# Correlation blocks of a convolution: gram matmuls in 32-column groups, two blocks per visit, and columns turned on VectorE

## The chip, the core and the metric

The kernel runs on one core of a Trainium2 chip. Time is device microseconds of one launch that processes all eight images: 2574.16 us, the median of three runs (2573.71 to 2581.83). One further execution was taken with the hardware profiler; the lines and times below come from it, in microseconds from its first instruction.

## The reference, cut to what matters

Two layers act on x of shape (8, 768, 32, 32). The first is a group norm, an attention whose scores come from the variances of keys and values, a projection and a residual. The second is a group norm, a convolution of 1x1 over the 768 channels and 28 correlation channels, and a residual. The change lies in the correlation channels:

```python
norm = jnp.sqrt(jnp.sum(feature * feature, axis=1, keepdims=True))
feat_n = feature / jnp.maximum(norm, EPS)
feat_pad = jnp.pad(feat_n, ((0, 0), (0, 0), (PAD, PAD), (PAD, PAD)))
corr = jnp.stack([jnp.sum(feat_pad[:, :, r:h + r, cc:w + cc] * feat_n, axis=1) for r, cc in _offsets()], axis=1)
x = jnp.concatenate([feature, corr], axis=1)
out = jnp.einsum('bchw,oc->bohw', x, conv_w) + conv_b[None, :, None, None]
```

For each pixel and each of 28 offsets (at most three rows and three columns away), corr is the dot product over 768 channels of the pixel's normalised feature with the neighbour's. Opposite offsets give the same products in another place, so 12 offsets and the pixel with itself are enough.

## The kernel before, in words

The program is written out in full when it is built, one instruction stream for each engine. The order is set by a planner: `Clock` keeps a modelled time, `later.after(us, job)` puts a job at a due time, `pass_time` runs what has come due, and every unit of TensorE work is emitted with its cost in microseconds (`KV_US` 1.93, `T_US` 2.58, `GRAM_US` 1.4). The planner only orders instructions; the engines wait for each other by semaphores, and each engine keeps its order. All loads and stores after the first go through SP's queue.

`work_off` mixes three sources: `rest` (units of the key and value projection of one image and the convolution of the image before), the attention steps (16 pairs of matmuls each, 6.9 us), and `beside`, which holds the correlation's gram blocks. A gram block is taken from `beside` by `next_to`, before and after each attention step and at places put into `rest`; `remaining` takes what is left before the last units of a projection. The wide products are made of matmuls with 64 weight columns, two side by side (`halves`, line 350), at seven products for eight.

The correlation of image b (class `Corr`, lines 1125 to 1254) runs in this order:

- `turn(t)`, lines 1128 to 1141: GpSimd copies block t of 128 tokens (four image rows) of f into a tile with the left and the right 16 columns of the image apart. Two operations a block. The pool `turnpool` has one buffer. Image 7 uses ScalarE and another pool.
- `gram(t)`, lines 1143 to 1180: for each of 6 channel chunks and each side, a matmul of 64 tokens (weights) with a window of 7 rows by 19 columns of the image, 133 moving columns; the last block has 4 rows, 76 columns. In float32 each matmul is two records in the trace. Then a copy to `win` by VectorE (ScalarE for image 7) and two DMAs a block into `windowed` in DRAM, whose row pitch makes the diagonals straight.
- `diagonals`, after blocks 3 and 7 (a half, 512 tokens): four DMAs bring the needed diagonals into `dd`.
- `scale`: norms (VectorE and GpSimd), then 20 columns for each of four blocks of 128 tokens, in `dn`.
- `to_dram` (line 1216 on): `dn` is turned by two TensorE products with an identity (`turned`, line 353, tile ct), copied by VectorE to `cr`, and stored to `rows` by four DMAs.
- `gather` (line 1231 on), after the second half: shifted copies of the rows come into `cs` and `v`, VectorE multiplies them, three DMAs copy the result to four groups of partitions, and `("cs", b)` is ready. `Wide.join` (line 1062) then adds the correlation's part to the convolution's products; image 7 has separate products for it (line 1373).

`KeysValues.spread(half)` (from line 704) makes the attention's scales after a half of the projection: small VectorE operations, one reduction over partitions on GpSimd, then rows to DRAM. At the start, `keep_warm` issues matmuls on an identity while the first image loads.

Of the kernel before, what the change touches and what calls it, by code (L numbers as in the profile page):

```python
# [27 lines left out]
RUNS = ((0, 0, 4), (31, -1, 3), (62, -2, 5), (93, -3, 7))  # L28
HW = W // 2
TALL, WIDE = MT // 2 + 3, HW + 3  # L30
AHEAD_OF = [o for first, _, count in RUNS for o in range(first, first + count)][1:]
NA = len(AHEAD_OF)
PAD = 99
# [20 lines left out]
TAIL = 0.0  # L54
EXP, SUM, STEP_US = 1.07, 1.15, 1.73
KV_US, T_US, CORR_US = 1.93, 2.58, 1.2
GRAM_US = 1.4
WARM, BRIDGE = 38, (3, 6)

# [32 lines left out]
class Clock:  # L92


    def __init__(self):
        self.now, self.count, self.jobs = 0.0, 0, []
        self.act, self.rows, self.poll = 0.0, ([], []), lambda: None
        self.dve = 0.0

    def after(self, us, job):  # L100
        self.count += 1
# [71 lines left out]
def two_layers(ctx, tc, x, wkv, wproj, bproj, wconv, wcorr, bconv, out):  # L173
# [14 lines left out]
    bcpool = pool("bcpool", 4)  # L188
    bkpool = pool("bkpool", 2)
    expool = pool("expool", 2 * AHEAD)  # L190
    turnpool = pool("turnpool", 1)
    wk = pool("wk", 3)
    uvpool = pool("uvpool", 1)
    st = pool("st", 1)
    xbank = pool("xbank", 2, space=PSUM)
    ybank = pool("ybank", 2, space=PSUM)
# [16 lines left out]
    def small(name):  # L213
        return other([P, 512], name)
# [238 lines left out]
    wins = [const.tile([P, WIN], F32, name=f"win{i}") for i in range(3)]  # L453
    for win in wins:
        nc.gpsimd.memset(win, 0.0)
    across = const.tile([W, NA], F32, name="across")

    def mask_rows():
        nc.gpsimd.memset(mask, 1.0)
# [135 lines left out]
    class KeysValues:  # L595
# [48 lines left out]
        def unit(self, half, d, n, g, p):  # L644
            b = self.b
            if n == 0:
                self.make_sums(half, (2 * d, 2 * d + 1))
            s = self.sums[g]
            a = {1: self.block(g, 0, 0), 2: self.block(g, 0, 1), 4: self.block(g, 1, 1)}
            a.update({5: s[:, 0], 6: s[:, 1], 7: s[:, 2], 3: s[:, 3]})  # L650
            w = kv_stream.tiles[b, half, d, p]
            pairs = [(a[p][:, k, :], w[:, k, :]) for k in range(JH)]
            taken = lambda ps: self.take(half, g, p, ps)
            if p == 2 and not b + half + d:
                ps = other([P, KW], f"z{g}")
                for k, (lhsT, rhs) in enumerate(pairs):
                    halves(ps, lhsT, rhs, start=k == 0, stop=k == len(pairs) - 1)
                later.after(KV_US + 0.1, lambda: taken(ps))
            else:
                banks.product(g, p, KV_US, KW, pairs, taken)  # L660
            if p not in [q for _, q in (PAIR if b + half + d else OPENING)[n + 1 :]]:
                kv_stream.done((b, half, d, p))
            if d == 1 and n == len(PAIR) - 1:
                self.over = half == 1
                more = 4.0 if half and not b else 0.0
                later.after(KV_US + 0.5 + more, lambda: later.after_dve(0.0, lambda: self.spread(half)))

        def stats(self, kind, half, t, src):
# [455 lines left out]
    class Corr:  # L1124
# [3 lines left out]
        def turn(self, t):  # L1128
# [7 lines left out]
            for side in range(2):  # L1136
                if last:
                    act_copy(0.5, to[:, :, side], rows[:, :, :, side, :])
                else:
                    half = rows[:, :, :, side, :]  # L1140
                    nc.gpsimd.tensor_tensor(to[:, :, side], half, windows(ones, ones.ap[0], (0, J), (HW, 4), (1, HW)), ALU.mult)  # L1141

        def gram(self, t):

            b = self.b
            tall = min(TALL, H - 4 * t)
            n = tall * WIDE
            if t not in self.turned:
                self.turn(t)
            block = self.turned[t]  # L1150
            ps = other([P, SPAN], f"gr{b}_{t}")
            for j in range(J):
                image = self.f[:, j, :].rearrange("p (y x) -> p y x", x=W)
                for side in range(2):
                    left = side * (HW - 3)
                    nc.tensor.matmul(  # L1156
                        ps[side * HD : (side + 1) * HD, :n].rearrange("p (y x) -> p y x", x=WIDE),
                        lhsT=block[:, j, side, :],
                        rhs=image[:, 4 * t : 4 * t + tall, left : left + WIDE],
                        start=j == 0, stop=j == J - 1,  # L1160
                    )
            for ahead in range(t + 1, min(t + (3 if b == NB - 1 else 2), MT)):
                if ahead not in self.turned:
                    self.turn(ahead)

            def out():
                win = wins[t % 2 if t < MT - 1 else 2]
                if b < NB - 1:
                    vector.tensor_copy(win[:, :n], ps[:, :n])
                else:  # L1170
                    act_copy(0.3, win[:, :n], ps[:, :n])
                for side in range(2):
                    to = windowed[b % 2][t : t + 1, side * (HD * PITCH + HD - 3) :]
                    nc.sync.dma_start(
                        out=windows(to, (HW * PITCH - 3, 4), (PITCH, HW), (1, WIN)), in_=win[side * HD : (side + 1) * HD, :]
                    )
                if t % 4 == 3:
                    later.after(4.0, lambda: self.diagonals(t // 4))

            later.after(GRAM_US + 0.25, out)  # L1180

        def diagonals(self, hf):

# [3 lines left out]
            for down, (_, right, count) in enumerate(RUNS):  # L1187
# [5 lines left out]
                    ),  # L1193
                )
                at += count
            later.after(6.0, lambda: self.scale(hf, dd))

        def scale(self, hf, dd):

# [4 lines left out]
            nc.gpsimd.tensor_tensor(rn, m, neghalf, ALU.pow)  # L1204

            def columns():
                dn = st.tile([P, 4, NROW], F32, tag="dn", name=f"dn{b}_{hf}")
                vector.tensor_copy(dn[:, :, 0], rn)
                for q in range(4):
                    vector.scalar_tensor_tensor(dn[:, q, 1:NROW], dd[:, q, :], rn[:, q : q + 1], mask, ALU.mult, ALU.mult)  # L1210
                later.after_dve(0.7 if b else 5.0 if hf else 7.5, lambda: to_dram(dn))

            def to_dram(dn):
                pt = small(f"ct{b}_{hf}")
                columns, over = dn.rearrange("p q r -> p (q r)"), 4 * NROW - HD
                turned(pt[0:HD, 0:P], columns[:, 0:HD])
                turned(pt[HD:P, 0:P], columns[:, over:])
                cr = work([P, P], f"cr{b}_{hf}")
                vector.tensor_copy(
                    cr.rearrange("k (y s x) -> k y s x", y=4, s=2),  # L1220
                    pt[:, 0:P].rearrange("k (s y x) -> k y s x", s=2, y=4),
                )
                for q in range(4):
                    at, row = PAD + hf * HF + q * P, q * NROW + (HD - over) * (q == 3)
                    nc.sync.dma_start(out=rows[b % 2][:, at : at + P], in_=cr[row : row + NROW, :])
                if hf == 1:
                    later.after(3.0, self.gather)

# [2 lines left out]
        def gather(self):  # L1231

            b, r = self.b, rows[self.b % 2]
            u = cs.rearrange("p a n -> p (a n)")[0:NCH, 0:N]
            v = uvpool.tile([NCH, N], F32, tag="uv", name=f"v{b}")
            nc.sync.dma_start(out=v[NS:NCH, :], in_=windows(r[0:1, PAD:], (0, NS + 4), (1, N)))
            nc.sync.dma_start(out=u[2 * NS : NCH, :], in_=windows(r[1:2, PAD:], (0, 4), (1, N)))
            for n, (first, apart) in enumerate(PICKED):
                k, row = 3 * n, 2 + AHEAD_OF.index(first)
                nc.sync.dma_start(out=u[k : k + 3, :], in_=windows(r[row : row + 1, PAD:], (apart * ROW, 3), (1, N)))  # L1240
                nc.sync.dma_start(out=v[k : k + 3, :], in_=windows(r[0:1, PAD + first :], (apart, 3), (1, N)))
                nc.sync.dma_start(
                    out=u[NS + k : NS + k + 3, :],
                    in_=windows(r[row : row + 1, PAD - first :], (apart * (ROW - 1), 3), (1, N)),
                )

            def product():
                vector.tensor_tensor(u, u, v, ALU.mult)
                vector.tensor_tensor(cs[0:NCH, 2, :], cs[0:NCH, 0, :], cs[0:NCH, 1, :], ALU.subtract)
                for n in range(1, 4):  # L1250
                    nc.sync.dma_start(out=cs[n * FOUR : n * FOUR + NCH, :, :], in_=cs[0:NCH, :, :])
                later.after_dve(6.0, lambda: ready.add(("cs", b)))

            later.after(18.0 if b < NB - 1 else 12.0, product)

    class Conv:

# [133 lines left out]

    def remaining(beside):
        while beside:
            next_to(beside)

    def next_to(beside):

        if beside and ready.issuperset(beside[0][1]):
            us, _, unit = beside.pop(0)
            unit()  # L1400
            clock.pass_time(us)
# [146 lines left out]
    for b in range(NB + 1):  # L1548
# [8 lines left out]
        if b:  # L1557
# [8 lines left out]
            if b < NB:  # L1566
# [6 lines left out]
            grams = [(GRAM_US if t < MT - 1 else 0.9, has_f if b > 1 else has_f + ("turned",), lambda t=t: (corr or corrs[0]).gram(t)) for t in range(MT)]  # L1573
# [71 lines left out]
```

## Time and profile before

| | us |
|---|---|
| median of three runs | 2574.16 |
| profiled execution | 2576.79 |
| its span, first to last instruction | 2575.1 |
| gram records (tile gr), 1536: TensorE busy | 103.49 |
| column turns (tile ct), 64: TensorE busy | 8.72 |
| denominators (tile den), 200: TensorE busy | 26.64 |
| GpSimd's turns, 112 of 384 elements | 110.7 |
| SP, windowed stores, 128: median of one issue | 0.52 |

The granted TensorE clock is full throughout. A row's busy time is the union of its records, and TensorE's records overlap: a matmul's record lasts from its start to a modelled end, while the next one starts long before that. What work takes away from TensorE's stream is therefore read from the starts in the timeline, not from busy times or means.

### The profile page before, as it was taken

The page shows a single profiled execution, that of the slowest core. Times are in us where ns is not written, and L with a number is a line of the kernel's source. Part 1 is how long each engine was busy: PE and PEld are TensorE (multiplying, and loading weights), DVE is VectorE, ACT ScalarE, POOL GpSimd, SP SyncE. Part 2 cuts the span into 40 slices and gives each one's busy share as a digit, 9 for nine tenths or more (in the row PEclk, how much of TensorE's full clock was granted, in tenths as well). Part 3 has the DMA queues.
Part 4 walks back from the last instruction along what each step waited for, and adds up shares of the span by engine and source line. Part 5 has one row for each costly group of instructions (what it writes and reads, how often), then busy time and mean ns, then how long its engine had stood idle before and what let it go on. Part 6 is the DMA issues. An engine that isn't in the chain of part 4 may idle for free.

```text
span 2575.1 us, 40595 instructions
## 1 busy us (share of the span) xinstructions
PE 2566.3 (100%) x14694; PEld 1246.2 (48%) x14694; DVE 1582.3 (61%) x4125; ACT 1417.5 (55%) x1972; POOL 422.4 (16%) x449
## 2 busy tenths in 40 slices
PE   9999999999999999999999999999999999999999
PEld 6545356334554347633476434664344333475333
DVE  6868735775447853478534785358853587535764
ACT  1497279811697217971179711897118971199610
POOL 4320130004300043000430003300133001331000
PEclk9999999999999999999999999999999999999999
DMA  8766366355563655636556365563655636445333
GB/s 293 293 220 229 102 212 186 120 198 170 185 190 116 198 168 178 205 98 206 169 176 202 97 212 169 168 204 100 218 166 174 207 107 218 151 158 167 119 109 109
DMA packets 331818, 448.56 MB, mean 174 GB/s; under 512 B 68431, under 2 KB 252623, under 8 KB 331619
## 3 DMA queue, kind: packets, MB, share of 16 engines
q1 hardware_dynamic: 329554, 442.62, 53.8%
q10 hardware_dynamic: 2064, 3.34, 0.4%
q8 instruction: 117, 1.92, 0.3%
q14 instruction: 83, 0.67, 0.1%
HBM read 376.70 MB, written 64.78 MB: 171 GB/s over the span
## 4 chain that ended last, share of the span: by engine, by line
PE 96%; DMA 2%; ACT 1%; DVE 1%; SPq 0%; issue 0%; POOL 0%; ACTq 0%; POOLq 0%; DVEq 0%
PE x L350 34%; PE av L801 25%; PE y L350 17%; PE z L350 10%; PE own L350 5%; PE gr L1156 3%; PE den L832 1%; ACT ex L775 1%; ACT junk L785 0%; DMA bk<-kdr 0%; DMA kv<-in_wkv_dram 0%; PE z L1062 0%; PE cc L1275 0%; PE y L1062 0%; DVE acc L167 0%
## 5 line engine op out<-in xcount | busy, mean ns | idle before, releaser
L775 ACT ACTIVATE ex<-bc,nk 128x1024 f32<-128x1024 f32 x768 | 826.9, 1139 | 382.4 <-DMA bc<-vdr 256.7
L801 PE MATMUL av<-ex,v 128*64 128x512 f32 x3072 | 699.8, 593 | 0.3 <-ACT ex L775 0.2
L801 PEld LDWEIGHTS av<-ex,v 128*64 128x64 f32 x3072 | 303.8, 137 | 355.3 <-issue 262.0
L785 ACT ACTIVATE junk<-bk,vm 128x1024 bf16<-128x1024 f32 x368 | 421.4, 1145 | 41.5 <-issue 17.8
L167 DVE TENSOR_TENSOR acc<-acc,ex 128x1024 f32<-128x1024 f32 x300 | 344.7, 1216 | 0.0
L350 PE MATMUL y<-kv,s 128*64 128x384 f32 x1488 | 265.6, 487 | 0.9 <-POOL s L636 0.9
L350 PE MATMUL x<-kv,xn 128*64 128x384 f32 x1512 | 261.4, 486 | 0.3 <-DMA kv<-in_wkv_dram 0.3
L350 PE MATMUL x<-kv,s 128*64 128x384 f32 x1488 | 256.2, 486 | 0.0
L229 ACT COPY kp<-x 128x384 f32<-128x384 f32 x28 | 13.4, 479 | 404.8 <-PE x L350 396.0
L350 PEld LDWEIGHTS x<-kv,xn 128*64 128x64 f32 x1512 | 134.2, 137 | 109.9 <-issue 83.9
L350 PEld LDWEIGHTS x<-kv,s 128*64 128x64 f32 x1488 | 131.6, 137 | 108.0 <-issue 87.1
L350 PEld LDWEIGHTS y<-kv,s 128*64 128x64 f32 x1488 | 130.1, 137 | 99.6 <-issue 75.3
L530 POOL TENSOR_TENSOR rstda<-vea,neghalf 128x1 f32<-128x1 f32 x8 | 4.8, 596 | 949.1 <-DVE vea L167 949.1
L1141 POOL TENSOR_TENSOR turn<-f,ones 128x384 f32<-128x384 f32 x112 | 110.7, 1010 | 242.1 <-PE gr L1156 182.2
L350 PE MATMUL z<-kv,xn 128*64 128x384 f32 x768 | 135.4, 486 | 0.0
L350 PE MATMUL x<-f,wt 128*64 128x512 f32 x504 | 120.0, 593 | 0.0
L167 DVE TENSOR_TENSOR v<-y,v 128x128 f32<-128x128 f32 x180 | 41.0, 283 | 124.1 <-PE y L350 124.1
L636 POOL TENSOR_TENSOR s<-xn 128x384 f32<-128x384 f32 x64 | 65.6, 1035 | 294.8 <-PE x L350 183.0
L167 DVE BATCH_NORM_STATS2 vbn<-v 128x6 f32<-128x64 f32 x720 | 101.7, 211 | 0.0
L167 DVE SCALAR_TENSOR_TENSOR xn<-x,bconv_sb,xn 128x512 f32<-128x512 f32 x63 | 46.5, 747 | 89.1 <-PE x L350 86.1
L229 ACT COPY acc<-li 32x256 f32<-32x256 f32 x128 | 51.6, 403 | 82.9 <-DVE li L167 81.5
L350 PEld LDWEIGHTS z<-kv,xn 128*64 128x64 f32 x768 | 72.6, 137 | 49.9 <-issue 36.0
(199 smaller groups left out, 3126.2 us busy)
## 6 DMA issues: line engine op xcount, KB each, us to landing
kv<-kvs SPq DMA_DIRECT2D x124, 576.0 KB
kv<-in_wkv_dram SPq DMA_DIRECT2D x95, 576.0 KB
bc<-vdr SPq DMA_DIRECT2D x96, 512.0 KB
f<-in_x_dram SPq DMA_DIRECT2D x48, 512.0 KB
bk<-kdr SPq DMA_DIRECT2D x46, 512.0 KB
x1d<-f SPq DMA_DIRECT2D x42, 512.0 KB
xn<-x1d SPq DMA_DIRECT2D x42, 512.0 KB
out_dram<-xn SPq DMA_DIRECT2D x82, 256.0 KB
```

Source lines behind the costliest of these rows:

```text
L167: return getattr(self.engine, name)(*args, **kw)
L229: nc.scalar.copy(to, at)
L350: nc.tensor.matmul(out[at], lhsT=lhsT[:, at], rhs=rhs, start=start, stop=stop, **kw)
L530: nc.gpsimd.tensor_tensor(self.rstd, ve, neghalf[:, 0:1], ALU.pow)
L636: nc.gpsimd.tensor_tensor(self.sums[g][:, 0], a[g][2], a[g][3], ALU.add)
L775: nc.scalar.activation(ex, self.bc[e], AF.Exp, scale=self.kv.nk[self.half][:, h, t : t + 1])
L785: nc.scalar.activation(junk, self.bk[e], AF.Exp, scale=self.kv.m2[self.half][:, h, t : t + 1], accum_out=self.sums[:, e, t : t + 1],)
L801: nc.tensor.matmul(self.av[hf][e * HD : (e + 1) * HD, :], lhsT=self.vt[:, t, e, :], rhs=exs[e][:, hf * HF : (hf + 1) * HF], start=t == 0, ...
L832: nc.tensor.matmul(den[at * 32 : (at + 1) * 32, :], lhsT=ones[:, 0:32], rhs=self.acc[e][:, hf * HF : (hf + 1) * HF], start=True, stop=True,)
L1141: nc.gpsimd.tensor_tensor(to[:, :, side], half, windows(ones, ones.ap[0], (0, J), (HW, 4), (1, HW)), ALU.mult)
L1156: nc.tensor.matmul(ps[side * HD : (side + 1) * HD, :n].rearrange("p (y x) -> p y x", x=WIDE), lhsT=block[:, j, side, :], rhs=image[:, 4 * ...
```

## The change

The gram of images 0 to 6 goes from two groups of 64 tokens to four of 32 tokens (two image rows by 16 columns), each with its own window of 5 rows by 19 columns (95 columns); in the last block all four take the same 4 rows. Image 7 keeps two groups. Blocks go two in a row (`grams`), with a gate in the planner (`clock.turned`) that holds the next pair until 5.8 us after the start of the last. Four DMAs store a block's windows where two did (two still in the last block). `turnpool` has two buffers, and both first blocks are turned when the correlation starts.

`dn` becomes a constant tile of 128 columns, four groups of 32; VectorE's 32 by 32 block transpose makes `cr` from it, so TensorE's two products and the copy out of PSUM go. Eight DMAs store a half's rows where four did. `v` is in two tiles, taken from `turnpool`, and loaded with twice the DMAs. The delays of `scale`, `to_dram` and the product are set anew, so is the place of image 0's second `spread` (8 us later), and there are five more warm matmuls at the start.

```diff
-GRAM_US = 1.4
-WARM, BRIDGE = 38, (3, 6)
+GRAM_US, TURN_US = (1.3, 2.4), 3.4
+WARM, BRIDGE = 42, (3, 7)
...
-                more = 4.0 if half and not b else 0.0
+                more = 12.0 if half and not b else 0.0
...
+        def grams(self, t):
+
+            clock.turned = clock.now + GRAM_US[1] + TURN_US
+            for n in range(2):
+                self.gram(t + n)
+
         def gram(self, t):
 
             b = self.b
-            tall = min(TALL, H - 4 * t)
+            last = t == MT - 1
+            groups = 2 if b == NB - 1 else 4
+            tall = min(SHORT if groups == 4 else TALL, H - 4 * t)
...
-                for side in range(2):
-                    left = side * (HW - 3)
+                each = P // groups
+                for at in range(groups):
+                    side, low = divmod(at, groups // 2)
+                    left, first = side * (HW - 3), 4 * t + (0 if last else 2 * low)
                     nc.tensor.matmul(
-                        ps[side * HD : (side + 1) * HD, :n].rearrange("p (y x) -> p y x", x=WIDE),
-                        lhsT=block[:, j, side, :],
-                        rhs=image[:, 4 * t : 4 * t + tall, left : left + WIDE],
+                        ps[at * each : (at + 1) * each, :n].rearrange("p (y x) -> p y x", x=WIDE),
+                        lhsT=block[:, j, side, low * each : (low + 1) * each],
+                        rhs=image[:, first : first + tall, left : left + WIDE],
                         start=j == 0, stop=j == J - 1,
                     )
-            for ahead in range(t + 1, min(t + (3 if b == NB - 1 else 2), MT)):
+            for ahead in range(t + 1, min(t + 3, MT)):
...
-                win = wins[t % 2 if t < MT - 1 else 2]
+                win = wins[t % 3 if t < MT - 1 else 3]
...
-                for side in range(2):
-                    to = windowed[b % 2][t : t + 1, side * (HD * PITCH + HD - 3) :]
+                whole = last or groups == 2
+                size, count, down = (WIN, 4, 0) if whole else (SHORT * WIDE + 3, 2, 2 * (HW * PITCH - 3 + WIDE))
+                for first in range(0, P, count * HW):
+                    side, low = divmod(first, HD)
+                    to = windowed[b % 2][t : t + 1, side * (HD * PITCH + HD - 3) + (down if low else 0) :]
                     nc.sync.dma_start(
...
-            later.after(GRAM_US + 0.25, out)
+            later.after(1.65 if b == NB - 1 else GRAM_US[t % 2] + 0.25, out)
...
-            later.after(6.0, lambda: self.scale(hf, dd))
+            later.after(13.0 if b < NB - 1 else 6.0, lambda: self.scale(hf, dd))
...
-                later.after_dve(0.7 if b else 5.0 if hf else 7.5, lambda: to_dram(dn))
+                later.after_dve(0.7 if b == NB - 1 else (5.0 if hf else 7.0) if b else 3.0 if hf else 6.0, lambda: to_dram(dn))
 
             def to_dram(dn):
-                pt = small(f"ct{b}_{hf}")
-                columns, over = dn.rearrange("p q r -> p (q r)"), 4 * NROW - HD
-                turned(pt[0:HD, 0:P], columns[:, 0:HD])
-                turned(pt[HD:P, 0:P], columns[:, over:])
                 cr = work([P, P], f"cr{b}_{hf}")
-                vector.tensor_copy(
...
+                vector.transpose(cr, dn.rearrange("p q r -> p (q r)"))
+                turned = cr.rearrange("p (q y x) -> p q y x", q=4, y=2)
+                for part in range(4):
+                    s, low = divmod(part, 2)
+                    for y in range(2):
+                        at = PAD + hf * HF + (2 * low + y) * W + s * HW
+                        nc.sync.dma_start(
+                            out=windows(rows[b % 2][0:1, at:], (ROW, NROW), (P, 4), (1, HW)),
+                            in_=turned[32 * part : 32 * part + NROW, :, y, :],
+                        )
...
-            v = uvpool.tile([NCH, N], F32, tag="uv", name=f"v{b}")
-            nc.sync.dma_start(out=v[NS:NCH, :], in_=windows(r[0:1, PAD:], (0, NS + 4), (1, N)))
+            vs = [turnpool.tile([P, J * P], F32, tag="turn", name=f"v{b}_{hf}") for hf in range(2)]
+            for hf, v in enumerate(vs):
+                nc.sync.dma_start(out=v[NS:NCH, :HF], in_=windows(r[0:1, PAD + hf * HF :], (0, NS + 4), (1, HF)))
...
-            later.after(18.0 if b < NB - 1 else 12.0, product)
+            later.after(20.0 if b < NB - 1 else 14.0, product)
...
     def remaining(beside):
         while beside:
+            clock.turned = 0.0
             next_to(beside)
...
-        if beside and ready.issuperset(beside[0][1]):
+        if beside and ready.issuperset(beside[0][1]) and clock.now >= clock.turned:
...
-        later.after(6.0, lambda: ready.add("turned"))
+        later.after(8.0, lambda: ready.add("turned"))
...
         corrs[-1].turn(0)
+        corrs[-1].turn(1)
...
-                for n in (3, 7) if b > 1 else (7, 11, 15):
+                for n in (3, 7) if b > 1 else (7,) + tuple(range(12, 30, 2)):
```

More of the change, by code (lines that the diff above doesn't have):

```diff
@@ L30 @@
 TALL, WIDE = MT // 2 + 3, HW + 3
+SHORT = 2 + 3
 AHEAD_OF = [o for first, _, count in RUNS for o in range(first, first + count)][1:]
@@ L97, in __init__ @@
         self.act, self.rows, self.poll = 0.0, ([], []), lambda: None
-        self.dve = 0.0
+        self.dve = self.turned = 0.0
     def after(self, us, job):
@@ L190, in two_layers @@
     expool = pool("expool", 2 * AHEAD)
-    turnpool = pool("turnpool", 1)
+    turnpool = pool("turnpool", 2)
     wk = pool("wk", 3)
-    uvpool = pool("uvpool", 1)
     st = pool("st", 1)
@@ L452, in two_layers @@
     windowed = [dconst.tile([MT, P * (PITCH + 2)], F32, name=f"windowed{i}") for i in range(2)]
-    wins = [const.tile([P, WIN], F32, name=f"win{i}") for i in range(3)]
+    wins = [const.tile([P, WIN], F32, name=f"win{i}") for i in range(4)]
     for win in wins:
@@ L456, in two_layers @@
     across = const.tile([W, NA], F32, name="across")
+    dns = [const.tile([P, 4, 32], F32, name=f"dn{n}") for n in range(2)]
+    for dn in dns:
+        nc.gpsimd.memset(dn, 0.0)
     def mask_rows():
@@ L1171, in out @@
                     act_copy(0.3, win[:, :n], ps[:, :n])
-                for side in range(2):
-                    to = windowed[b % 2][t : t + 1, side * (HD * PITCH + HD - 3) :]
+                whole = last or groups == 2
[3 more added lines that the diff above has]
+                    to = windowed[b % 2][t : t + 1, side * (HD * PITCH + HD - 3) + (down if low else 0) :]
                     nc.sync.dma_start(
-                        out=windows(to, (HW * PITCH - 3, 4), (PITCH, HW), (1, WIN)), in_=win[side * HD : (side + 1) * HD, :]
+                        out=windows(to, (HW * PITCH - 3, count), (PITCH, HW), (1, size)),
+                        in_=win[first : first + count * HW, :size],
                     )
@@ L1206, in columns @@
             def columns():
-                dn = st.tile([P, 4, NROW], F32, tag="dn", name=f"dn{b}_{hf}")
+                dn = dns[hf]
                 vector.tensor_copy(dn[:, :, 0], rn)
@@ L1210, in columns @@
                     vector.scalar_tensor_tensor(dn[:, q, 1:NROW], dd[:, q, :], rn[:, q : q + 1], mask, ALU.mult, ALU.mult)
-                later.after_dve(0.7 if b else 5.0 if hf else 7.5, lambda: to_dram(dn))
+                later.after_dve(0.7 if b == NB - 1 else (5.0 if hf else 7.0) if b else 3.0 if hf else 6.0, lambda: to_dram(dn))
             def to_dram(dn):
-                pt = small(f"ct{b}_{hf}")
-                columns, over = dn.rearrange("p q r -> p (q r)"), 4 * NROW - HD
-                turned(pt[0:HD, 0:P], columns[:, 0:HD])
-                turned(pt[HD:P, 0:P], columns[:, over:])
                 cr = work([P, P], f"cr{b}_{hf}")
-                vector.tensor_copy(
[L1220 to L1225, printed above, removed]
+                vector.transpose(cr, dn.rearrange("p q r -> p (q r)"))
[8 more added lines that the diff above has]
+                        )
                 if hf == 1:
@@ L1240, in gather @@
                 nc.sync.dma_start(out=u[k : k + 3, :], in_=windows(r[row : row + 1, PAD:], (apart * ROW, 3), (1, N)))
-                nc.sync.dma_start(out=v[k : k + 3, :], in_=windows(r[0:1, PAD + first :], (apart, 3), (1, N)))
+                for hf, v in enumerate(vs):
+                    nc.sync.dma_start(out=v[k : k + 3, :HF], in_=windows(r[0:1, PAD + first + hf * HF :], (apart, 3), (1, HF)))
                 nc.sync.dma_start(
@@ L1247, in product @@
             def product():
-                vector.tensor_tensor(u, u, v, ALU.mult)
+                for hf, v in enumerate(vs):
+                    vector.tensor_tensor(cs[0:NCH, hf, :], cs[0:NCH, hf, :], v[0:NCH, :HF], ALU.mult)
                 vector.tensor_tensor(cs[0:NCH, 2, :], cs[0:NCH, 0, :], cs[0:NCH, 1, :], ALU.subtract)
@@ L1572, in two_layers @@
                 conv.then = low_residual
-            grams = [(GRAM_US if t < MT - 1 else 0.9, has_f if b > 1 else has_f + ("turned",), lambda t=t: (corr or corrs[0]).gram(t)) for t in range(MT)]
+            if b < NB:
+                keys = has_f if b > 1 else has_f + ("turned",)
+                grams = [(GRAM_US[1], keys, lambda t=t: (corr or corrs[0]).grams(t)) for t in range(0, MT, 2)]
+            else:
+                grams = [(1.4 if t < MT - 1 else 0.9, has_f, lambda t=t: corr.gram(t)) for t in range(MT)]
             first, start = (0.0, has_f, conv.sums.first), (0.0, (), conv.start)
```

## The prediction

> **What bounds the kernel.** First the page's busy shares, then its chain of waits: is one engine the bound, and with what? (Engine, busy us, share of the span, instructions; then the chain's shares by engine and by line.)
>
> ```profile
> PE 2566.3 (100%) x14694; PEld 1246.2 (48%) x14694; DVE 1582.3 (61%) x4125; ACT 1417.5 (55%) x1972; POOL 422.4 (16%) x449
> ...
> PE 96%; DMA 2%; ACT 1%; DVE 1%; SPq 0%; issue 0%; POOL 0%; ACTq 0%; POOLq 0%; DVEq 0%
> ```
>
> TensorE holds the whole chain, so every microsecond of matmul stream taken out of it counts and work on other engines counts only where TensorE comes to wait. What a matmul occupies is not its row's mean (278 ns for a gram matmul), since matmuls overlap, but the distance between starts. That is read from the timeline of image 1's correlation (start, duration, engine, line, operation, count):
>
> ```profile
> 655.96 4.04 PE L350 MATMUL x<-kv,s 128*64 128x384 f32 x24
> 659.83 1.59 PE L1156 MATMUL gr<-f,turn 128*64 128x133 f32 x24
> 661.19 2.16 PE L350 MATMUL y<-kv,s 128*64 128x384 f32 x12
> ...
> 692.55 1.59 PE L1156 MATMUL gr<-f,turn 128*64 128x133 f32 x24
> 693.91 0.45 PE L353 MATMUL ct<-ident,dn 128*64 128x128 f32 x4
> 694.12 2.16 PE L350 MATMUL z<-kv,xn 128*64 128x384 f32 x12
> ...
> 712.03 1.02 PE L1156 MATMUL gr<-f,turn 128*64 128x76 f32 x24
> 712.82 3.45 PE L350 MATMUL x<-kv,s 128*64 128x384 f32 x20
> ```
>
> A gram block costs 661.19 - 659.83 = 1.36 us, the last of an image 0.79, a column turn (ct) 0.21. Each block is 24 matmul records, two column groups side by side: 12 rounds of 0.113 us at 133 columns, 0.066 at 76. The 384-column unit gives 3.87 / 12 = 0.3225 a round. Over the three widths that is 0.00083 us a column and next to nothing fixed: the stream is bound by columns alone, and two groups run at the price of one.
>
> **Gram in four groups (images 0 to 6).** Removed: 7 images x (7 x 1.36 + 0.79) = 72.2 us. Put in: each block is still 12 rounds, now of four groups with 5 rows x 19 = 95 columns: 0.066 + 19 x 0.00083 = 0.082 us a round, 0.98 a block. The last block keeps 76 columns and 0.79. Sum: 7 x (7 x 0.98 + 0.79) = 53.6, **18.6 us less**. This needs four 32-column groups to stream at once. The denominators' matmuls are the row for that, the only 128x32 form before:
>
> ```profile
> 248.45 4.05 PE L350 MATMUL z<-kv,xn 128*64 128x384 f32 x24
> 252.43 1.07 PE L832 MATMUL den<-acc,ones 128*32 128x512 f32 x8
> 253.43 16.28 PE L801 MATMUL av<-ex,v 128*64 128x512 f32 x63
> ```
>
> Eight of them, two rounds, take 253.43 - 252.43 = 1.00 us; two rounds of 512 columns by the law above are 2 x 0.4294 = 0.86. So four groups do run side by side, and 0.14 is lost on the way back to 64-column groups. On the way in, 12 rounds of 384 from 248.45 end at 252.32, and den starts at 252.43: 0.11 more. The first 512-column unit after another den (276.21 to 278.84) takes 2.63 instead of 6 x 0.4294 = 2.58: 0.05. That is 0.30 a visit, more where the two 64-column streams run out of step and one has to wait for the other; I take 0.33, with 0.2 and 0.45 as ends. The change makes the visits in pairs of blocks: 7 x 4 = 28 visits, **9.2 us given back** (5.6 to 12.6).
>
> **A rule that speaks against it.** The row first: den's eight records span 1.07 us, each 0.605 long by its group, second round 0.43 later, so four starts fall within some 0.03 us, below 10 ns each. The new gram needs a start every 0.082 / 4 = 0.0204 us, 96 times in a pair. The Trainium skill (TensorE: Matmul & The Clock Gate, section "Wait — 56ns, not 53.3ns?") says that starts never come closer than about 25 ns however small the matmul; its Part 3 gives about 4 ns between groups packed in one array. The trace bears out the second for four in a burst, and nothing shorter than 33 ns for a sustained run (0.79 / 24). By the first rule a block is 48 x 0.025 = 1.20 us and the gram becomes 7 x 8 x 1.20 + 9.2 = 76.4, **4.2 more** than before; by the row it is 53.6 + 9.2 = 62.8, **9.4 less**. I take the row, because it is the same form of matmul, and keep the rule as a rival.
>
> **Column turns on VectorE.** Sixteen ct of 0.21 us leave TensorE: **3.4 us**. VectorE's 128x128 copy out of PSUM (4.67 us for 16) becomes one 128x128 transpose in SBUF; the nearest row, the 128x32 transpose, takes 0.17 to 0.21 us, and VectorE at 61% has room for anything up to a microsecond. Costed at nothing. One PSUM bank fewer is asked for.
>
> **Transfers.** All on SP. Per image 0 to 6: 7 blocks x 2 more windowed issues at 0.52 us, 8 more rows at 0.32, 5 more v at 0.27, 11 us in 318 us; SP's own instructions fill 856 of 2575 us. What queues behind them are weight loads held five and seven blocks ahead. Hidden; uncovered, it would be a kv load late by a burst (8 windowed issues, 4 us) against five blocks that last two units, 3.9 us, each. The rows' pieces shrink from 512 to 64 bytes, a form the trace lacks; nobody waits for it but the correlation.
>
> **The correlation's due time.** Delays grow by 7.0 before scale, 4.3 before the turn (images 1 to 6, second half) and 2.0 before the product: 13.3 us. In image 1, cs was copied at 756.8 to 759.4 and first read at 778.9, about 19 us of cover. And the pairs come sooner: places that took one block now take two, so at 652.7, about 661, 671 and 680 by the units between them, instead of ending at 712. Nothing is late.
>
> **Turns on GpSimd.** Four operations of 1.01 us now stand together after each pair. The first two can start when the first block ends (1.1 us after the pair's start), so all end at about 5.3; the new gate holds the next pair to 5.8. No wait is added. In image 0 blocks came 3.8 us apart and waited, 0.24 and 0.23 us; the gate ends these: **0.5 less**.
>
> **Image 0's later spread.** It moves eight VectorE operations and a reduction out of the way of the last pieces of image 1's normalisation, which GpSimd's sums and then TensorE stand for. The only wait it can free is
>
> ```profile
> 159.15 2.16 PE L350 MATMUL y<-kv,s 128*64 128x384 f32 x12 [0.89 <-POOL s L636]
> ```
>
> **0.9 less** (0 to 0.9). Its own result is due when pair 3's exponentials begin, about 190; it was at hand near 165, and 8 us later still is.
>
> **Warm-up and tail.** Five more warm matmuls: the first group ended at 12.83 with 13.62 next, and four more end at 13.7; the bridge ends before the weights land at 16.86. **+0.2** (0 to 0.3). Image 7 keeps two groups. Its chain to the last correlation gets 2.0 us longer: copies issued at 2550.1 to 2552.7 come to about 2555, with some 2 to landing, and the first reader stood at 2557.17. **+0.5** (0 to 1.5).
>
> **Sum.** -18.6 + 9.2 - 3.4 - 0.5 - 0.9 + 0.2 + 0.5 = -13.5. The profiled execution took 2576.8 (span 2575.1 and 1.7 around it), giving 2563.3; it lies 2.6 above the median of 2574.2, and the change starts from that median: **2561**. With all ends one way: 2556 to 2566.
>
> **Rivals.** *Issue floor:* 25 ns a start, as above: +4.2 - 3.4 - 1.4 + 0.7 = +0.1, **2574**. For it: no sustained run below 33 ns is seen. Against: den's burst, and matmuls queued behind long ones beforehand. *Turns behind sums (slower):* in image 1 GpSimd spends 696.2 to 703.9 on the four sums of a projection and turns nothing. A turn that queues behind them ends at 1.1 + 7.7 + 4.0 = 12.9 us after its pair, the next pair may come at 8.2, so TensorE waits about 5. Once an image that is 35 us: 2561 + 35 = **2596**; from 3 us an image the change is no faster. Against: by the places above the pairs are done before the sums begin; only image 0 (sums at 375.7) comes within a few microseconds. *The groups do not run side by side* but two at a time: 7 x (7 x 1.96 + 1.58) = 107 + 9 - 72 = +44, **2618**; den's row speaks against it.
>
> **Chances.** A measurement of this kernel tells 0.3% (7.7 us) from no change. Forecast 0.74, issue floor 0.14, turns behind sums 0.09, no packing 0.03. The forecast's own range lies wholly on the faster side, the floor in the middle, the others slower. Range 2556 to 2574: the forecast's own and the floor's.
>
> **What would show it.** Right: gram blocks near 1.0 us from start to start within a pair, about 0.3 lost around each pair, no ct on TensorE, TensorE still without waits. The floor shows as starts 25 ns apart and pairs of 2.7 us; the sums as waits of gram for turn; a late cs as waits of the joined matmuls (L1062 before) for cs.

## The result, and the profile after

The changed kernel takes 2595.77 us in the median of six runs (2592.85 to 2602.11), the kernel before beside it 2576.94 (six runs, 2573.71 to 2581.83). The ratio is 1.0076, with an interval of 1.0066 to 1.0086: slower by 0.8%, where 0.5% faster was forecast. The profiled execution took 2593.92, its span is 2592.2.

First the page: engines with busy us, share and instructions; then the chain of waits by engine and by line.

```profile
PE 2572.7 (99%) x15984; PEld 1080.0 (42%) x15984; DVE 1595.7 (62%) x4133; ACT 1415.5 (55%) x1972; POOL 423.1 (16%) x452
...
PE 90%; ACT 5%; DVE 2%; issue 2%; DMA 1%; SPq 0%; POOL 0%; ACTq 0%; DVEq 0%; POOLq 0%
PE x L350 33%; PE av L804 22%; PE y L350 16%; PE z L350 10%; PE own L350 5%; ACT ex L778 3%; PE gr L1169 2%; ACT junk L788 2%; PE den L835 1%; PE warm L419 1%; DMA bk<-kdr 1%; DVE acc L168 0%; DVE v L168 0%; DVE xn L168 0%; PE z L1065 0%
```

TensorE had 96% of the chain and has 90%; ScalarE went from 1% to 5%. Three names in the last line tell the story before any detail: ex (the attention's exponentials), junk (ScalarE's passes for the denominators, named for their unused output) and the DMA bk<-kdr that feeds them. Then TensorE's waits (for whom, us in all, times, longest):

```profile
PE av L804 <- ACT ex L778: 11.5, 14, 2.3
PE warm L419 <- POOL ident masks.py:199: 1.6, 1, 1.6
PE gr L1169 <- issue: 1.5, 1, 1.5
PE x L350 <- DVE t2o L168: 0.6, 1, 0.6
```

Before, attention (av) waited 0.2 us for the exponentials in the whole span; now it waits 11.5. The line of before:

```profile
PE av L801 <- ACT ex L775: 0.2, 1, 0.2
```

The place is the timeline of image 1, here from its second pair of gram blocks on (start, duration, engine, line, operation, count, wait):

```profile
656.55 4.04 PE L350 MATMUL x<-kv,s 128*64 128x384 f32 x24
660.52 2.17 PE L1169 MATMUL gr<-f,turn 128*32 128x95 f32 x96
662.62 2.16 PE L350 MATMUL y<-kv,s 128*64 128x384 f32 x12
664.61 4.04 PE L350 MATMUL x<-kv,s 128*64 128x384 f32 x24
668.58 2.17 PE L1169 MATMUL gr<-f,turn 128*32 128x95 f32 x96
670.67 5.37 PE L804 MATMUL av<-ex,v 128*64 128x512 f32 x24
677.18 2.97 PE L804 MATMUL av<-ex,v 128*64 128x512 f32 x8 [1.14 <-ACT ex L778]
680.08 1.98 PE L1169 MATMUL gr<-f,turn 128*32 128x95 f32 x96
```

The gram did what was forecast: from 660.52 the next unit after a pair starts 2.10 us later, where two separate blocks took 2.72. Then the first attention step has its 32 matmul records from 670.67 to 680.08, 9.41 us; 16 rounds at 0.4294 are 6.87. In the kernel before, the same step ran from 670.29 to 677.15, 6.86:

```profile
670.29 7.09 PE L801 MATMUL av<-ex,v 128*64 128x512 f32 x32
677.15 1.59 PE L1156 MATMUL gr<-f,turn 128*64 128x133 f32 x24
```

So 2.5 us are lost in one step, and the row names only 1.14 of them as a wait. The single records explain the difference. Each tile of exponentials belongs to one of the pair's two heads, and each head is one of the two 64-column streams. At 677.18 and 677.66 only the first head's stream runs, on the seventh tile, which has just been made. The second stream needs the eighth, which ScalarE makes 1.04 us after the seventh; it starts at 678.22, together with the first stream's next matmul, which stands behind it in TensorE's order. The last two records, at 679.13 and 679.55, are the second stream's alone. **The step ends by its last tile, and the list of waits names only the time in which TensorE is wholly idle**, not the wait of one stream while the other runs.

Over the span, TensorE's stream (every matmul's columns at the law's price) fell by 21.0 us, and yet the span grew by 17.1. So it holds 38.1 us more beyond the stream: 28 visits at 0.29 account for 8.1, and 30 are lost time that the forecast did not have. Most of it is in the attention's matmuls: from their starts to the next units' they take 29.2 us more than their columns' price, where it was 4.2 before.

Why are the exponentials late? SP's queue, in the kernel before and then after, at the same place (start, duration, queue, line, transfer, count):

```profile
656.63 1.10 SPq L1174 DMA_DIRECT2D windowed<-win  x2
657.83 5.05 SPq L593 DMA_DIRECT2D kdr<-rsk  x2
662.93 1.01 SPq L306 DMA_DIRECT2D kv<-in_wkv_dram  x2
664.04 1.10 SPq L1174 DMA_DIRECT2D windowed<-win  x2
665.19 1.10 SPq L764 DMA_DIRECT2D bk<-kdr  x2
```

```profile
656.47 2.84 SPq L1190 DMA_DIRECT2D windowed<-win  x4
659.37 3.97 SPq L596 DMA_DIRECT2D kdr<-rsk  x2
663.44 2.51 SPq L1190 DMA_DIRECT2D windowed<-win  x4
666.06 0.92 SPq L306 DMA_DIRECT2D kv<-in_wkv_dram  x2
667.03 2.56 SPq L1190 DMA_DIRECT2D windowed<-win  x4
669.64 1.00 SPq L767 DMA_DIRECT2D bk<-kdr  x2
```

bk is the row of key scales for the first pair of heads; it goes out 4.45 us later, behind twelve windowed stores, 7.91 us in all, instead of four, 2.20 us. (kdr is where the row lies in DRAM; the second of its two transfers waits for the first to land.) ScalarE, before and then after:

```profile
659.78 6.56 ACT L775 ACTIVATE ex<-bc,nk 128x1024 f32<-128x1024 f32 x6 [27.58 <-DMA bc<-vdr]
671.69 1.15 ACT L785 ACTIVATE junk<-bk,vm 128x1024 bf16<-128x1024 f32 x1 [5.35 <-DMA bk<-kdr]
...
672.84 4.25 ACT L775 ACTIVATE ex<-bc,nk 128x1024 f32<-128x1024 f32 x4
```

```profile
660.92 6.56 ACT L778 ACTIVATE ex<-bc,nk 128x1024 f32<-128x1024 f32 x6 [29.02 <-DMA bc<-vdr]
674.84 1.15 ACT L788 ACTIVATE junk<-bk,vm 128x1024 bf16<-128x1024 f32 x1 [7.36 <-issue]
...
675.99 4.25 ACT L778 ACTIVATE ex<-bc,nk 128x1024 f32<-128x1024 f32 x4
```

ScalarE does six exponentials, then has a denominators' pass in its order, which needs bk. (The row of after calls the wait "issue"; in the trace, the semaphore of bk's first load reaches its count at 674.77, and the pass starts at 674.84.) The seventh exponential stands behind that pass: 675.99 instead of 672.84. TensorE's first step uses eight tiles of exponentials and reaches the seventh at about 675.8. So the chain is: stores, bk, junk, ex, av. The kernel before had some 0.5 us to spare on it: its eighth exponential ended at 675.01, and the matmul that reads it started at 675.50.

### The profile page after: what moved, and what is told of

It is laid out like the page before. It is cut to its first block, busy times and chain, and to the rows that moved or that the text cites. A ratio compares the mean times of both kernels' runs of the same rounds, so it can differ in the third digit from the quotient of the medians.

```text
span 2592.2 us, 43459 instructions
## 1 busy us (share of the span) xinstructions
PE 2572.7 (99%) x15984; PEld 1080.0 (42%) x15984; DVE 1595.7 (62%) x4133; ACT 1415.5 (55%) x1972; POOL 423.1 (16%) x452
## 4 chain that ended last, share of the span: by engine, by line
PE 90%; ACT 5%; DVE 2%; issue 2%; DMA 1%; SPq 0%; POOL 0%; ACTq 0%; DVEq 0%; POOLq 0%
PE x L350 33%; PE av L804 22%; PE y L350 16%; PE z L350 10%; PE own L350 5%; ACT ex L778 3%; PE gr L1169 2%; ACT junk L788 2%; PE den L835 1%; PE warm L419 1%; DMA bk<-kdr 1%; DVE acc L168 0%; DVE v L168 0%; DVE xn L168 0%; PE z L1065 0%
## 5 line engine op out<-in xcount | busy, mean ns | idle before, releaser
L804 PE MATMUL av<-ex,v 128*64 128x512 f32 x3072 | 734.5, 594 | 11.8 <-ACT ex L778 11.5
L804 PEld LDWEIGHTS av<-ex,v 128*64 128x64 f32 x3072 | 237.5, 137 | 464.6 <-issue 380.6
L350 PE MATMUL y<-kv,s 128*64 128x384 f32 x1488 | 276.8, 488 | 0.0
L350 PE MATMUL x<-kv,xn 128*64 128x384 f32 x1512 | 273.5, 486 | 0.0
L350 PE MATMUL x<-kv,s 128*64 128x384 f32 x1488 | 264.0, 486 | 0.0
L350 PEld LDWEIGHTS y<-kv,s 128*64 128x64 f32 x1488 | 124.9, 137 | 105.3 <-issue 89.1
L350 PE MATMUL z<-kv,xn 128*64 128x384 f32 x768 | 140.6, 486 | 0.0
L350 PE MATMUL x<-f,wt 128*64 128x512 f32 x504 | 134.7, 592 | 0.0
```

What stands on the lines that cost most here:

```text
L350: nc.tensor.matmul(out[at], lhsT=lhsT[:, at], rhs=rhs, start=start, stop=stop, **kw)
L804: nc.tensor.matmul(self.av[hf][e * HD : (e + 1) * HD, :], lhsT=self.vt[:, t, e, :], rhs=exs[e][:, hf * HF : (hf + 1) * HF], start=t == 0, ...
```

## The experiments

Two theories stood at the start. *Queue:* the added stores delay bk, as above. *Planner:* the planner's new costs (a pair 2.4, turns 3.4) misplace the work around the pairs. Beside every set of runs the kernel before measured 2576.8 to 2577.6.

**1. bk on another queue.** Everything of the change stays; for images 1 to 7 the first pair's bk loads go through ScalarE's queue.

```diff
-            nc.sync.dma_start(out=bc, in_=windows(...))
+            queue = nc.scalar if kind == "k" and self.hp == 0 and self.b else nc.sync
+            queue.dma_start(out=bc, in_=windows(...))
```

> The changed kernel, but the two loads of the denominators' rows (bk) of the first attention pair go out on ScalarE's own queue instead of SP's. Theory Q (SP's queue): these loads stand behind 12 windowed stores where 4 stood before, ScalarE starts the denominators 3 us later, and TensorE waits about 3.4 us for exponentials in the first two attention steps of each of 7 images; with the loads moved, that goes: 2596 - 24 = about 2572, between 2566 and 2580. Theory P (the planner): it counts 2.4 us for a pair of blocks that takes 2.2, so TensorE runs ahead of the plan and finds the exponentials unfinished; the queue is no matter, and the time stays above 2588.

Measured 2570.50 (13 runs, 2569.62 to 2573.60), ratio to before 0.9972 (0.9963 to 0.9980): 25 us faster than the changed kernel. ScalarE's timeline, with its queue in it:

```profile
663.35 0.81 ACTq L768 DMA_DIRECT2D bk<-kdr  x2
664.20 4.27 ACT L779 ACTIVATE ex<-bc,nk 128x1024 f32<-128x1024 f32 x4 [0.21 <-ACT ex L779]
668.65 1.15 ACT L789 ACTIVATE junk<-bk,vm 128x1024 bf16<-128x1024 f32 x1 [0.17 <-DMA bk<-kdr]
...
673.40 4.26 ACT L779 ACTIVATE ex<-bc,nk 128x1024 f32<-128x1024 f32 x4 [3.52 <-PE av L805]
```

The pass starts at 668.65, and the next exponentials wait for TensorE to free their buffers and no longer for bk. TensorE's waits for exponentials fall from 11.5 us to one:

```profile
PE av L805 <- ACT ex L779: 2.0, 1, 2.0
```

**2. The same in the kernel before** (before_bk_queue), to see whether the queue is a gain of its own.

> A control: the kernel before, with the first pair's bk loads on ScalarE's queue. In the kernel before these loads came in time, so theory Q has no wait to remove: 2577 within 4 us. If the move itself were worth the 25 us that it brought after the change, the time would be near 2552.

2574.45 (12 runs), ratio 0.9993 (0.9985 to 1.0002). No gain that can be told. So the 25 us are what the change had cost, and no gain of the other queue.

**3. The planner's costs.**

```diff
-GRAM_US, TURN_US = (1.3, 2.4), 3.4
+GRAM_US, TURN_US = (1.2, 2.1), 3.7
```

> The changed kernel with the planner's costs set to what the trace shows: 1.2 for the first block, 2.1 for the pair, the gate kept at 5.8 us. Theory P: the order comes right, 2572 to 2585. Theory Q: the stores still stand ahead of the loads, so 2591 to 2600.

2597.06, ratio 1.0076 (1.0061 to 1.0091): as the changed kernel. The waits fall otherwise (av waits 19.7 us, in seven places), but the loss stays. The planner theory falls, as far as these costs go.

**4. Three times the stores in the kernel before.** Each windowed store of images 0 to 6 is issued three times, with the same data to the same place.

```diff
-                for side in range(2):
+                for side in (0, 1) * (3 if b < NB - 1 else 1):
```

> The kernel before, with each windowed store of images 0 to 6 issued three times (the same data to the same place), so that 12 stores stand ahead of the first pair's bk loads as in the changed kernel, and nothing else is changed. Theory Q: these loads go out some 4 us later and TensorE waits as it does after the change: slower by 15 to 25 us, 2592 to 2602. Theory P: nothing to do with the queue, 2577 within 4 us.

2713.49, ratio 1.0527 (1.0511 to 1.0543): far past what was expected, and by another mechanism. SP's waits show it:

```profile
SPq L1174 <- DMA windowed<-win: 243.6, 119, 7.5
```

In this program a store to a place that an earlier one writes waits, by a semaphore, for the earlier one's landing, up to 7.5 us. That measures repeated writes, not three issues, so it decides nothing.

**5 and 6. More stores, disjoint.** The kernel before with its two stores a block cut into six, and into eight, each to a place of its own: 12 and 16 of them ahead of bk. The edit for eight (for six the list is ((0, 2), (2, 1), (3, 1))):

```diff
-                    nc.sync.dma_start(out=windows(to, (HW * PITCH - 3, 4), ...), in_=win[side * HD : (side + 1) * HD, :])
+                    for y, count in ((0, 1), (1, 1), (2, 1), (3, 1)) if b < NB - 1 else ((0, 4),):
+                        at = side * (HD * PITCH + HD - 3) + y * (HW * PITCH - 3)
+                        to, p = windowed[b % 2][t : t + 1, at:], side * HD + y * HW
+                        nc.sync.dma_start(out=windows(to, (HW * PITCH - 3, count), ...), in_=win[p : p + count * HW, :])
```

> The kernel before, with the windows of each block of images 0 to 6 in six stores that don't overlap, where two did it (the same data): 12 stores ahead of the first pair's bk loads, as after the change, but with no store waiting for another, as the three-fold stores did. Theory Q: bk goes out some 4 us later, ScalarE starts the denominators 3 us later, TensorE waits in the first attention steps: slower by 12 to 30 us, 2589 to 2607. If the stores were no matter: 2577 within 4 us.

> The kernel before, with the windows of each block of images 0 to 6 in eight stores that don't overlap (one for each image row and side, the same data): 16 stores ahead of the first pair's bk loads. With six stores a block ScalarE began the denominators 1.2 us later and the time grew by 3 us, as good as nothing; after the change it began 3.4 us later and TensorE waited. Theory Q with a threshold (some 2 us of slack in front of the fourth pair of exponentials): now bk goes out 5 to 6 us later than before, ScalarE starts 3 us later, and the time grows by 12 to 30 us, 2589 to 2607. If the queue costs nothing, or grows evenly with the stores: 2577 to 2583.

Six: 2579.82 (20 runs), ratio 1.0012 (1.0005 to 1.0018), a miss. Eight: 2599.67, ratio 1.0090 (1.0073 to 1.0107), as expected. Times in image 1 (us after the first gram) make one line of the four kernels:

| | stores ahead | bk issued | first junk | seventh ex | av waits, all images |
|---|---|---|---|---|---|
| before | 4 | 12.5 | 19.0 | 20.2 | 0.2 |
| six stores | 12 | 15.0 | 19.5 | 20.7 | 1.0 |
| the change | 12 | 17.2 | 22.4 | 23.5 | 11.5 |
| eight stores | 16 | 17.5 | 22.6 | 23.8 | 13.5 |

TensorE's waits in the two, six first:

```profile
PE av L801 <- ACT ex L775: 1.0, 2, 0.6
```

```profile
PE av L801 <- ACT ex L775: 13.5, 8, 3.1
```

The loss follows the pass, not bk's issue. bk 2.5 us later moves the pass by only 0.5, because the pass there starts 4.5 us after that issue instead of 6.5 (why bk lands sooner stays open), and 0.5 us is about what the kernel before could spare; the run is 3 us longer. bk 5 us later moves the pass by 3.6, and the run is 22 us longer. For bk's issue, what counts is SP's time ahead of it, not the number of stores: the change's twelve take 2.84 + 2.51 + 2.56 = 7.91 us, the twelve of the six-store kernel only 3.14 + 3.12 = 6.26, since most of them are of one image row (median of an issue 0.42 against 0.57), and the two kdr transfers between them, which took 5.05 us before, shrink to 3.97 and 3.27. Stores and kdr together are 7.25 before, 9.53 with six, 11.88 in the change and 12.20 with eight (9.69 and 2.51): 2.3, 4.6 and 5.0 more, which is bk's delay in the table within 0.2. With eight stores and nothing else of the change, the kernel before becomes as slow as the changed one: such a delay of the queue is enough to make the loss.

**7. The turn alone.** The kernel before with VectorE's turn, the constant tile and eight row stores; gram, stores and delays as before.

```diff
-                turned(pt[0:HD, 0:P], columns[:, 0:HD])
-                turned(pt[HD:P, 0:P], columns[:, over:])
...
+                vector.transpose(cr, dn.rearrange("p q r -> p (q r)"))
...
+                        nc.sync.dma_start(out=windows(rows[b % 2][0:1, at:], ...), in_=turned[32 * part : 32 * part + NROW, :, y, :])
```

> The kernel before with one part of the change alone: columns turned by VectorE's block transpose into one constant tile, eight row stores a half, the delays as before. Both theories: TensorE loses 16 times 0.21 us, 3.4 us faster, 2573 to 2574; if the stores of 64-byte pieces were to come late to the gather, the wait would stand at the joined matmuls and the time above 2580.

2584.16 (nine runs), ratio 1.0030 (1.0019 to 1.0042): a miss. SP's queue in image 2's attention, before and then with the turn:

```profile
1069.44 6.70 SPq L593 DMA_DIRECT2D vdr<-rsv  x2
...
1079.48 1.08 SPq L764 DMA_DIRECT2D bc<-vdr  x2
```

```profile
1071.15 9.47 SPq L596 DMA_DIRECT2D vdr<-rsv  x2
...
1083.96 1.08 SPq L767 DMA_DIRECT2D bc<-vdr  x2
```

bc, the row of value scales, goes out 4.5 us later. TensorE itself is 1.7 us behind by then, and vdr's first transfer goes out just as much later; the other 2.77 are vdr's 9.47 us instead of 6.70. Its second transfer waits for the first to land, and that comes 2.3 us after the last landing of the gather's copies in both kernels (1075.54 after 1073.26, and 1080.01 after 1077.77). The gather stands behind the eight row stores (3.49 us together, the four took 1.42) and the transfers after them. So ScalarE starts late, and TensorE waits:

```profile
1109.65 3.86 PE L804 MATMUL av<-ex,v 128*64 128x512 f32 x7 [2.77 <-ACT ex L778]
```

It is another row of the attention that comes late by the same queue, here by a landing. In the change, where scale and turn are due later, this wait is not seen: bk_other_queue's trace has a single wait of av, in image 0.

**8. The turn alone, the gather 9 us later.**

```diff
-                    later.after(3.0, self.gather)
+                    later.after(12.0 if b < NB - 1 else 3.0, self.gather)
```

> The turn alone, as before, but the gather is begun 9 us later (image 7's as before), so that the attention's value rows (vdr) of the second half go out ahead of it on SP's queue and not behind it. If turn_alone lost its 3.4 us and 7 more to that order, the waits of 2.8 to 3.3 us for exponentials go, and the time is 2573 to 2576. If the 64-byte stores themselves are the cost, it stays at 2580 to 2590.

2580.33 (20 runs), ratio 1.0010 (1.0004 to 1.0017). Half right: from image 1's first gram to image 6's it takes 1584.6 us against 1589.6 before, with no wait for exponentials there. But image 0 now loses some 9.6 us, with such waits of 6.3 us in all, the longest 4.1.

**9. The grams alone.** bk_other_queue with its columns turned by TensorE as before (ct, four row stores).

> The changed kernel with bk on ScalarE's queue (2570.5), and the columns turned by TensorE as before, with four row stores a half: what VectorE's turn is worth where nothing is late. By the sum of the prediction 16 times 0.21 us: 3.4 us slower, 2574. If TensorE's time there is covered by waits for ScalarE, within 1.5 us of 2570.5.

2574.87 (12 runs), ratio 0.9991 (0.9982 to 0.9999). Against 2570.50, the turn on VectorE is worth 4.4 us by the medians. The two traces don't show where: the profiled executions took 2572.75 and 2573.60, and from image 1's first gram to image 6's bk_other_queue is only 0.7 us the shorter.

**10. One block a visit.** bk_other_queue with each block as a visit of its own, eight an image, at 1.25 in the planner.

```diff
-                grams = [(GRAM_US[1], keys, lambda t=t: (corr or corrs[0]).grams(t)) for t in range(0, MT, 2)]
+                grams = [(1.25, keys, lambda t=t: (corr or corrs[0]).gram(t)) for t in range(MT)]
```

> The changed kernel with bk on ScalarE's queue (2570.5), and the blocks taken one at a time as before, not in pairs: 28 more visits to the 32-column form. At 0.29 us a visit, as the trace of the changed kernel has it, 8.1 us slower: 2578 to 2579. If going in and out of the form cost nothing, within 2 us of 2570.5.

2661.25, ratio 1.0331 (1.0314 to 1.0349), a miss by 80 us. A single visit costs what was expected (1.12 us from its start to the next unit's, 0.10 ahead of it and 0.05 in the unit after: 0.29 over 0.98), but image 1's last gram comes at 717, where pairs had it at 680. The reading that fits is that with the longer delays the correlation is late, and the convolution's units that stand behind it are missing between the attention steps. TensorE waits for ScalarE:

```profile
PE av L805 <- ACT ex L779: 45.1, 17, 4.1
PE av L805 <- ACT v L229: 8.5, 6, 2.3
```

The halved clock (last section) adds to it; in this trace it lasts 41 us in all. So the pairs matter for when the correlation comes, more than for the visits that they save.

**11. Image 0's later spread taken back.** In the changed kernel, `more = 4.0` as before.

> The changed kernel with image 0's second spread back at its place (4.0 instead of 12.0). The wait of 0.89 us of TensorE for GpSimd's sums near 159 us comes back: 2596.7; within 3 us of the changed kernel in any case.

2594.88, ratio 1.0074 (1.0059 to 1.0089): no difference to the changed kernel. The wait of y for GpSimd's sums, 0.9, comes back in its trace, and the end does not move with it.

**12. Attention steps up to 1 us later.** bk_other_queue stands above the forecast; is TensorE reaching the steps too soon?

```diff
-            return self.made >= self.done + AHEAD and self.exp_at <= clock.now + 1.0
+            return self.made >= self.done + AHEAD and self.exp_at <= clock.now
```

> The changed kernel with the first pair's bk loads on ScalarE's queue (bk_other_queue, 2570.5) and one constant of the planner different: an attention step may start when the planner's own clock says that its exponentials are there, no longer up to 1.0 us before. bk_other_queue stands some 9 us above the forecast sum. If that rest is TensorE reaching the attention steps just ahead of the exponentials, so that its two column streams fall a round out of step, steps that start up to 1.0 us later with projection rounds put ahead of them give 2563 to 2568, and the waits of av for ex (2.0 us in all) go. If the rest is that the projection rounds run out ahead of the steps, pushing the steps later makes it worse: 2572 or more. If neither matters, 2570 to 2571.

2602.17 (five runs), ratio 1.0095 (1.0081 to 1.0110). TensorE's waits:

```profile
PE x L350 <- DVE t2o L168: 21.6, 5, 4.7
PE x L350 <- DVE xn L168: 4.3, 5, 0.9
PE av L805 <- ACT ex L779: 1.7, 1, 1.7
```

Projection rounds moved ahead of the steps reach t2o, a sum of the convolution's, before VectorE has made it. This is the "runs out" side of the expectation. From image 3's first gram to image 4's it takes 324.0 us, bk_other_queue 317.7. Of these 6.3, the waits there (4.65 for t2o, 0.85 for xn) and a halved clock after the longer one (1.3, last section) make 6.8. Away from them the later start gains 0.5 us, of some 1.4 by which an image of bk_other_queue falls short of the forecast (it takes 0.5 less than before, where 3.1 of stream less and 1.2 of visits more make 1.9).

## Why the prediction was wrong

The forecast sum was -13.5; the profiled execution came out 17.1 longer.

- **The step that failed** is "Transfers. All on SP. [...] What queues behind them are weight loads held five and seven blocks ahead. Hidden". The count of instructions and their price were about right (0.57 us a store in the median, 0.52 forecast). Wrong was what stood behind them: not only weight loads but the attention's bk and bc rows, which ScalarE needs within microseconds. "Uncovered" was priced at one kv load; it was 25 us (experiment 1). The view that would have shown it was at hand: SP's own timeline from the first gram on, with bk at 665.19, the pass that waited 5.35 us for bk, and av, which starts on its eighth exponential 0.5 us after that one ends.
- **Gram in four groups:** right. 18.6 us of stream went, at 0.98 a block. The rule of a floor near 25 ns between starts (the Trainium skill, "TensorE: Matmul & The Clock Gate", section "Wait — 56ns, not 53.3ns?") does not hold here for starts in four column groups: a block's 48 starts in 0.98 us are 20.4 ns apart in the mean (four within 0.02 us, the next four 0.08 us after these began), as that page's Part 3 lets one expect. The rival *issue floor* is out, and so is *not side by side*.
- **Visits:** at 0.29, as the pairs of image 1 have it, 28 are 8.1; forecast 9.2. They pay 0.10 on the way in, 0.14 on the way out, 0.05 in the next unit.
- **Column turns on VectorE:** forecast 3.4, measured 4.4 by the medians (experiments 1 and 9). The transpose takes 0.300 us. But the row stores that come with it are not free: with the delays of before, the turn and its stores make the kernel 7 us slower (experiment 7).
- **The correlation's due time:** "nothing is late" holds for the change. It holds only with pairs (experiment 10).
- **Turns on GpSimd:** no wait of TensorE for a turn is left, so *turns behind sums* was not the cause; that it forecast 2596, nearly the measured time, is chance. The two waits for turn (0.5) went, but a wait of 1.5 us, released by nothing that the profile names, stands in image 0's gram.
- **Image 0's later spread:** its wait of 0.9 went, and nothing came of it at the end (experiment 11).
- **Warm-up:** the first weights' matmul starts at 17.02 instead of 16.86; +0.2 was forecast. **Tail:** the first reader of cs comes at 2574.42 instead of 2557.17, 17.25 later, and the end 17.1 later: no wait was added there, where 0.5 was forecast.

With bk out of the way, the change gives 2570.50 beside 2577.29, -6.8, half of the forecast. Where the other half went is settled only in part. In the traces, that kernel's span holds 17.8 us more beyond its stream than the kernel before, of which visits are 8.1; but its profiled execution is the slowest of its 13, 3.1 above their median. Some 3.5 of the other 10 are in image 0, where av waits 2.0 once and the clock is halved for 3.41 us after it. The rest is some 1.4 us an image, at the joins and denominators after a step whose two streams start apart. One such step can be followed in image 2. ScalarE ends its tiles at 1079.7 and 1080.8, one stream starts on the first at 1079.85, the other on the second at 1080.82, and it stays one matmul behind until the join; in the kernel before the same step runs in its 6.86 us. ScalarE is busy for 42.7 of the 43 us from 1040 to 1083 (42.5 before): there TensorE, rid of grams, only comes to the exponentials sooner. That this makes up the rest fits, but experiment 12 didn't bear it out, and it stays a guess.

bk_other_queue beats both kernels: 0.28% below the one before, just within what was called no change.

## What to carry to other kernels

Before adding transfers to a shared queue, list by time what stands behind them, and for each how long its reader still has; "the queue is a third busy" says nothing of that. The slack of a load is read at its reader and at the reader's own queue: a pass that waits for bk holds every exponential behind it. And when a part of a change brings waits of its own, move one transfer to an idle queue as the first experiment, since it parts the compute from its transport in one line.

## What the runs showed of the hardware

**A wait of TensorE can cost more than itself.** The clock that was granted to TensorE after the wait of 4.22 us in step_later, which ended at 876.33 (window, length, TensorE busy and count, clock, DMA share, GB/s):

```profile
875.00:876.00 1.00, 0.00 (x0) 0.80 0.00 0
876.00:877.00 1.00, 0.67 (x2) 0.50 0.00 0
877.00:878.00 1.00, 1.00 (x4) 0.50 0.00 0
878.00:879.00 1.00, 1.00 (x6) 0.50 0.00 0
879.00:880.00 1.00, 1.00 (x8) 0.99 0.08 23
```

The clock is halved for some 3.4 us, of which 2.66 are work; that is 1.3 us more. The Trainium skill (the page named above, section "What's actually happening") has the clock fall after an idle window of about 3.4 us. Here the length of a wait alone does not decide. Waits of 2.77, 2.90 and 3.07 us had the fall, and one of 2.02 in bk_other_queue:

```profile
461.00:462.00 1.00, 1.00 (x4) 0.50 0.08 16
```

One of 2.29 in the changed kernel and one of 3.67 in before_three_stores had none. In the changed kernel's profiled execution the clock is full, so the loss read from its trace has no part of this; in its other five runs the mean clock is 0.997 to 0.999, so these have some of it.

**Two column streams can run one matmul apart.** In bk_other_queue's image 2 the second stream is 0.86 us behind from 1080.82 on. The join at 1095.55 starts when both are through, and the two last rounds before it, at 1094.60 and 1095.03, are of one stream alone. No wait stands in the trace for this, since TensorE is never wholly idle.
